# A spiking recommender scan: spikes counted on VectorE instead of TensorE, the comparison fed by ScalarE, item 0's rows made five steps at a time

## The chip, the core and the metric

The kernel runs on one core of one Trainium2 chip. The metric is the device time of one execution in microseconds, the median over several runs. It was 1573.67 us before the change (5 runs, 1573.37 to 1573.87).

## What is computed

There are 1024 sequences (B) of 50 item numbers (T). Each item has a row of D = 128 numbers in a table of 100001 rows. Row 0 counts as zeros.

```python
emb = emb_table.at[0].set(0.0)
prefix = jnp.cumsum(emb[seq], axis=1)
denom = jnp.minimum(arange(1, T + 1)[None, :], lengths[:, None])
uF = prefix / denom[:, :, None]
mean = uF.mean(axis=0)
var = uF.var(axis=0)
y = (uF - mean) * lax.rsqrt(var + 1e-5) * gamma + beta
def step(v, x):                       # over the 50 steps, v starts at 0
    v = v + (x - v) / 2.0
    spike = (v - 1.0 >= 0)
    return v - spike * 1.0, spike
scores = spikes.mean(axis=0) @ emb.T  # 1024 x 100001, float32
```

The output alone is 409.6 MB.

## The kernel before

The kernel has two parts. The first, lines 164 to 406, is the scan over 50 steps. The second, from line 411, multiplies the counts of spikes by the whole table and stores the scores. `tc.manual_schedule()` is in force, so each engine executes its instructions in the order in which the program writes them.

**The scan.** Features lie on the 128 partitions and the 1024 sequences along the free axis. For each step t, `gather` (L191) issues eight indirect DMAs on GpSimd's queue (POOL), 128 rows each, into one of three buffers `e`. It is called two steps ahead: the loop calls `gather(t + 2)`. Eight transposes on TensorE (L301) add the gathered rows to `pre`, two PSUM banks that hold the running sum. Each half (512 sequences) is scaled by VectorE into `uF` (L310), and `bn_stats` (L311) takes its statistics; `bn_aggr` (L321) joins the two halves in `mv`.

Then comes the normalization. ScalarE takes the square root (L325) and subtracts the mean from `uF` in place (L326). VectorE takes the reciprocal `r` (L334), refines it by a Newton step (L336 to L338) and forms the factor `a` (L340). `x` (L344) is a ScalarE operation that writes the scaled input into a new PSUM tile `v`, and `step` (L347) on VectorE subtracts half of the negated old potential `negv`.

The spike of step t - 1 is computed in step t: `s` (L331) is v >= 1 in bfloat16, `negv` (L353) is s - v, and `counted` (L268) adds `s` to two PSUM banks `sums` by two matmuls with an identity. In the last step these are written ahead of everything else (L295, L296), then counted, and `sums` is copied to an SBUF tile `count` (L319).

**Item 0.** Rows of item 0 were gathered and must be taken out of the sum again. `only(t)` (L252, ScalarE) makes a stationary operand `l` that keeps only row t, and `correct(t, l)` (L257) multiplies it by a mask `zT` into `pre`. Step t calls `correct(t + 1, l)` and later `only(t + 2)`.

**The end of the scan.** After the last step sixteen transposes of the identity (`warm`, L378) are put on TensorE's queue ahead of the products. The last membrane step is done in three column groups (L385 to L393), and `spiked` (L279) adds the last spikes to `count` as it writes `countA`, `countB` and `countC`, the stationary operands of the second part. Two first blocks of scores (L397 to L406) are multiplied into `sums` and `po1`, then scaled and stored.

**The second part.** Blocks of the table (1024 rows each) are transposed and split into a high and a low float32r part (`prepare`). Each product needs two matmuls per 512 columns (L152), one eviction by VectorE (L469) or ScalarE (L471), and stores on SyncE's queue. In steps 42 and 44 of the scan the first two blocks are already prepared.

Of the kernel before, what the change touches and what calls it, by code (L numbers as in the profile page):

```python
# [12 lines left out]
F32 = mybir.dt.float32  # L13
BF16 = mybir.dt.bfloat16
F32R = mybir.dt.float32r
I32 = mybir.dt.int32
U32 = mybir.dt.uint32
AF = mybir.ActivationFunctionType
ALU = mybir.AluOpType

P = 128
BN_EPS = 1e-5
V_TH = 1.0
HALF = 1024
KQ = HALF // P
BANK = 512
GROUP = 6
AHEAD = 6
TWICE = 2

WIDTHS = 4 * [2] + 4 * [3] + 13 * [6]
# [4 lines left out]
def rec_kernel(  # L36
# [9 lines left out]
    nc = tc.nc  # L46
    B, T = seq.shape
    N, D = table.shape
# [19 lines left out]
    ident = const.tile([P, P], F32, tag="ident", name="ident")  # L68
# [80 lines left out]
    def product(po, q, n, k0, kw):  # L149
        kw += kw % 2  # L150
        for j, part in enumerate(split[q]):
            nc.tensor.matmul(  # L152
                po[:, :kw],
                lhsT=counts[n],
                rhs=part[:, k0 : k0 + kw],
                start=j == 0,
                stop=j == 1,
            )
# [4 lines left out]

    with ExitStack() as ph:
        once = ph.enter_context(tc.tile_pool(name="once", bufs=1))
        lp = ph.enter_context(tc.tile_pool(name="lif", bufs=2))
        sp = ph.enter_context(tc.tile_pool(name="stats", bufs=3))
        up = ph.enter_context(tc.tile_pool(name="uF", bufs=2))
        gp = ph.enter_context(tc.tile_pool(name="gather", bufs=3))
        accp = ph.enter_context(tc.tile_pool(name="acc", bufs=1, space=bass.MemoryType.PSUM))  # L170
# [8 lines left out]
        gb = once.tile([P, 2], F32, tag="gb", name="gb")  # L179
# [32 lines left out]
        zT = once.tile([P, B], F32R, tag="zT", name="zT")  # L212
# [3 lines left out]
        r0n = once.tile([P, D], F32, tag="r0n", name="r0n")  # L216
# [3 lines left out]
        sel = once.tile([P, P // 2], F32, tag="sel", name="sel")  # L220
# [11 lines left out]
        nc.vector.tensor_copy(rlen, rps)  # L232

        hgb = once.tile([P, 2], F32, tag="hgb", name="hgb")
        nc.vector.tensor_scalar_mul(hgb[:, 0:1], gb[:, 0:1], -0.5)
        nc.vector.tensor_scalar_mul(hgb[:, 1:2], gb[:, 1:2], 0.5)
        eps = once.tile([P, 1], F32, tag="eps", name="eps")
        nc.vector.memset(eps, BN_EPS)
        ident_h = once.tile([P, P], BF16, tag="ident_h", name="ident_h")
        nc.vector.tensor_copy(ident_h, ident)  # L240

        negv = once.tile([P, B], F32, tag="negv", name="negv")
        nc.vector.memset(negv, 0.0)


        pre = [accp.tile([P, BANK], F32, tag=f"pre{h}", name=f"pre{h}") for h in range(B // BANK)]
        sums = [accp.tile([P, BANK], F32, tag=f"sums{h}", name=f"sums{h}") for h in range(B // BANK)]

        def only(t):

            l = sp.tile([P, D], F32R, tag="l", name=f"l_{t}")
            nc.scalar.activation(l, r0n, AF.Copy, scale=sel[:, t : t + 1])  # L252
            return l

        def correct(t, l):
            for h in range(B // BANK):
# [6 lines left out]
                    skip_group_check=True,  # L263
                )

        def counted(t, s):
            for h in range(B // BANK):
                nc.tensor.matmul(  # L268
                    sums[h],
                    lhsT=ident_h,  # L270
                    rhs=s[:, h * BANK : (h + 1) * BANK],
                    start=t == 0,
                    stop=t == T - 2,
                    skip_group_check=True,
                )


        def spiked(out, cs, v):
            nc.vector.scalar_tensor_tensor(out, v, V_TH, count[:, cs], ALU.is_ge, ALU.add)  # L279

        whole = slice(0, B)
        halves = [slice(h * BANK, (h + 1) * BANK) for h in range(B // BANK)]
        v = None

        correct(0, only(0))
        l = only(1)
        gather(1)
        for t in range(T):
            last = t == T - 1
            if t + 2 < T:  # L290
                gather(t + 2)
            e = es.pop(t)
            if last:
                s = lp.tile([P, B], BF16, tag="s", name=f"s_{t - 1}")
                nc.vector.tensor_single_scalar(s, v, V_TH, ALU.is_ge)  # L295
                nc.vector.tensor_tensor(negv, s, v, ALU.subtract)  # L296
            uF = up.tile([P, B], F32, tag="uF", name=f"uF_{t}")
            bs = sp.tile([P, B // BANK, 6], F32, tag="bs", name=f"bs_{t}")
            for h, cs in enumerate(halves):
                for k in range(0, BANK, P):  # L300
                    nc.tensor.matmul(  # L301
                        pre[h][:, k : k + P],
                        lhsT=e[:, h * BANK + k : h * BANK + k + P],
                        rhs=ident,
                        start=False,
                        stop=last,
                        is_transpose=True,
                        skip_group_check=True,
                    )
                nc.vector.scalar_tensor_tensor(uF[:, cs], rlen[:, cs], 1.0 / (t + 1), pre[h], ALU.max, ALU.mult)  # L310
                nc.vector.bn_stats(bs[:, h, :], uF[:, cs])  # L311
            if not last:
                correct(t + 1, l)
            else:

                counted(t - 1, s)
                count = once.tile([P, B], F32, tag="zT", name="count")
                for h, cs in enumerate(halves):
                    nc.scalar.copy(count[:, cs], sums[h])  # L319
            mv = sp.tile([P, 2], F32, tag="mv", name=f"mv_{t}")  # L320
            nc.vector.bn_aggr(mv, bs.rearrange("p h s -> p (h s)"))  # L321


            r = sp.tile([P, 1], F32, tag="r", name=f"r_{t}")
            nc.scalar.activation(r, mv[:, 1:2], AF.Sqrt, bias=eps)  # L325
            nc.scalar.activation(uF, uF, AF.Identity, bias=mv[:, 0:1], scale=-1.0)  # L326


            if t and not last:
                s = lp.tile([P, B], BF16, tag="s", name=f"s_{t - 1}")  # L330
                nc.vector.tensor_single_scalar(s, v, V_TH, ALU.is_ge)  # L331
                counted(t - 1, s)

            nc.vector.reciprocal(r, r)  # L334
            q = sp.tile([P, 1], F32, tag="q", name=f"q_{t}")
            nc.vector.tensor_mul(q, r, r)  # L336
            nc.vector.scalar_tensor_tensor(q, mv[:, 1:2], BN_EPS, q, ALU.add, ALU.mult)
            nc.vector.tensor_scalar(q, q, -0.5, 1.5, ALU.mult, ALU.add)  # L338
            a = sp.tile([P, 1], F32, tag="a", name=f"a_{t}")
            nc.vector.tensor_scalar(a, q, r, hgb[:, 0:1], ALU.mult, ALU.mult)  # L340


            def x(vt, cs):
                nc.scalar.activation(vt, uF[:, cs], AF.Identity, bias=hgb[:, 1:2], scale=a)  # L344

            def step(vt, cs):
                nc.vector.scalar_tensor_tensor(vt, negv[:, cs], -0.5, vt, ALU.mult, ALU.add)  # L347

            if not last:
                vt = vp.tile([P, B], F32, tag=f"v{t % 2}", name=f"v_{t}")  # L350
                x(vt, whole)
                if t:
                    nc.vector.tensor_tensor(negv, s, v, ALU.subtract)  # L353
                step(vt, whole)
                v = vt
                if t + 2 < T:
                    l = only(t + 2)

                if t in (T - 8, T - 6):
                    q = (t - T + 8) // 2  # L360
                    pair(q)
                    prepare(q, vp.tile([P, HALF], F32, tag="v1", name=f"pt_{q}"))
                    if q == TWICE - 1:
                        for k in range(TWICE):
                            rows[GROUP + k] = first[:, k, :]
                        nc.sync.dma_start(
                            out=first[:, :TWICE, :],
                            in_=table[GROUP * HALF : (GROUP + TWICE) * HALF, :].rearrange(
                                "(q p k) d -> p q (k d)", p=P, k=KQ
                            ),  # L370
                        )
# [21 lines left out]
            spiked(c, cs, vt)  # L393


        po1 = vp.tile([P, HALF], F32, tag="v0", name="po_0_1")
        for q, (pool, tag, po) in enumerate(((gp, "e", sums), (up, "uF", [po1[:, cs] for cs in halves]))):  # L397
            o = pool.tile([P, HALF], F32, tag=tag, name=f"o_0_{q}")
            for h, cs in enumerate(halves):
                product(po[h], q, 0, h * BANK, BANK)  # L400
            for h, cs in enumerate(halves):
                if q and h:
                    nc.vector.tensor_scalar_mul(o[:, cs], po[h], 1.0 / T)
                else:
                    nc.scalar.mul(o[:, cs], po[h], 1.0 / T)
                store(0, q * HALF + h * BANK, o[:, cs])  # L406


# [102 lines left out]
```

## Time and profile before

| What | Value |
|---|---|
| median of 5 runs | 1573.67 us (1573.37 to 1573.87) |
| the profiled execution | 1574.11 us |
| its span, first to last instruction | 1572.3 us |
| outside the span | 1.81 us |
| TensorE busy in the span | 1148.2 us (73%) |
| VectorE busy | 941.7 us (60%) |
| ScalarE busy | 631.3 us (40%) |
| GpSimd busy | 378.3 us (24%) |
| mean granted TensorE clock | 0.945 |
| DMA, mean over the span | 310 GB/s |

In the profile's lines PE is TensorE, DVE is VectorE, ACT is ScalarE, POOL is GpSimd and PEld is TensorE's loading of weights. A timeline row gives the start, the duration (both in us), the engine, the line, the operation, output<-input, and in brackets the idle time of that engine just before, with what ended it. A row of a group of instructions gives the total busy time in us and the mean of one in ns, and then the idle time before them. PEclk is the clock granted to TensorE as a share of full speed.

### The profile page before, as it was taken

Reading aid. Unit: us, or ns where it says so; the run is one execution under the profiler, and the core shown is the slowest. Engines: PE = TensorE matmul, PEld = TensorE weight load, DVE = VectorE, ACT = ScalarE, POOL = GpSimd, SP = SyncE. Lnnn points to the kernel's source line nnn. Section 1 sums busy time; section 2 is a strip of 40 time slices with the busy share of each in tenths; the row PEclk is TensorE's granted clock in tenths of the full one; section 3 lists DMA queues with packets and bytes.
Section 4 is the critical chain, followed back from the end, with each engine's and each line's share of the span. In section 5 each row is a group of like instructions: output and inputs, shape, how many; then the busy total and the mean of one; then the engine's idle time right before and its main releaser. Section 6 shows DMA issues by size and latency. Waiting matters only on the chain.

```text
span 1572.3 us, 12553 instructions
## 1 busy us (share of the span) xinstructions
PE 1148.2 (73%) x4538; PEld 818.2 (52%) x4548; DVE 941.7 (60%) x1161; ACT 631.3 (40%) x700; POOL 378.3 (24%) x406
## 2 busy tenths in 40 slices
PE   4555555555546998889888878888788878888884
PEld 2222222222223776668666666666566667666673
DVE  5777777777778665667555545545555545555552
ACT  2322222222233554555444444444344444444542
POOL 7777777777776000000000000000000000000000
PEclk9999999999975999999999999999999999899998
DMA  9611111111121999999999999999999999999997
GB/s 339 247 52 54 52 54 52 54 52 54 52 80 44 385 416 403 423 416 403 419 432 431 430 424 425 417 416 433 425 426 414 408 429 418 419 415 429 406 432 338
DMA packets 53691, 488.14 MB, mean 310 GB/s; under 512 B 11995, under 2 KB 12796, under 8 KB 32380
## 3 DMA queue, kind: packets, MB, share of 16 engines
q1 hardware_dynamic: 32256, 429.81, 65.1%
q0 software_dynamic: 12800, 26.24, 5.7%
q10 hardware_dynamic: 8572, 31.28, 5.0%
q8 instruction: 36, 0.59, 0.1%
q14 instruction: 27, 0.22, 0.0%
HBM read 77.69 MB, written 409.60 MB: 310 GB/s over the span
## 4 chain that ended last, share of the span: by engine, by line
DMA 56%; POOL 17%; PE 9%; issue 8%; ACT 5%; DVE 3%; another core or an unknown queue 0%; ACTq 0%; SPq 0%; DVEq 0%; POOLq 0%
DMA scores<-o 50%; POOL e L194 17%; PE po L152 8%; DMA e<-in_L_rec_emb_table,idx 6%; ACT o L471 5%; DVE o L469 2%; PE pre L301 0%; DVE s L331 0%; DVE bs L311 0%; DVE uF L310 0%; ACT pairs L144 0%; DMA idx<-in_r_seq 0%; PE pt L122 0%; PE sums L268 0%
## 5 line engine op out<-in xcount | busy, mean ns | idle before, releaser
L469 DVE TENSOR_SCALAR o<-po 128x1024 f32<-128x1024 f32 x391 | 464.4, 1221 | 349.6 <-DMA scores<-o 313.5
L471 ACT ACTIVATE o<-po 128x1024 f32<-128x1024 f32 (+1 forms) x391 | 389.2, 1018 | 542.4 <-DMA scores<-o 324.2
L194 POOL DMA_INDIRECT e<-in_L_rec_emb_table,idx x400 | 377.7, 944 | 124.0 <-issue 110.6
L152 PE MATMUL po<-pairs,countB 128*128 128x512 f32 x1136 | 304.3, 414 | 61.4 <-ACT o L471 46.1
L152 PEld LDWEIGHTS po<-pairs,countB 128*128 128x128 f32 x1136 | 217.4, 196 | 124.3 <-ACT o L471 61.2
L152 PE MATMUL po<-pairs,countC 128*128 128x512 f32 x852 | 233.5, 420 | 51.4 <-ACT o L471 51.3
L301 PE MATMUL pre<-ident,e 128*128 128x128 f32 x400 | 156.1, 452 | 151.7 <-DMA e<-in_L_rec_emb_table,idx 148.0
L152 PEld LDWEIGHTS po<-pairs,countC 128*128 128x128 f32 x852 | 164.6, 200 | 96.8 <-ACT o L471 63.4
L301 PEld LDWEIGHTS pre<-ident,e 128*128 128x128 f32 x400 | 79.2, 200 | 245.2 <-DMA e<-in_L_rec_emb_table,idx 222.9
L145 DVE TENSOR_TENSOR pairs<-pt,pairs 128x1024 fp32r<-128x1024 f32 x71 | 86.2, 1222 | 91.7 <-ACT pairs L144 91.6
L325 ACT ACTIVATE r<-mv,eps 128x1 f32<-128x1 f32 x50 | 14.8, 295 | 305.5 <-DVE mv L321 305.5
L310 DVE SCALAR_TENSOR_TENSOR uF<-rlen,pre 128x512 f32<-128x512 f32 x100 | 68.4, 684 | 108.3 <-PE pre L301 108.2
L122 PE MATMUL pt<-ident,rows 128*128 128x128 f32 x782 | 111.4, 289 | 5.3 <-issue 3.2
L122 PEld LDWEIGHTS pt<-ident,rows 128*128 128x128 f32 x782 | 100.8, 152 | 24.1 <-issue 9.4
L152 PE MATMUL po<-hi,countB 128*128 128x512 f32 x216 | 88.8, 411 | 19.9 <-ACT o L471 14.9
L257 PE MATMUL pre<-zT,l 128*128 128x512 f32 x100 | 77.4, 776 | 19.5 <-DVE uF L310 19.3
L268 PE MATMUL sums<-s,ident_h 128*128 128x512 bf16 x88 | 45.3, 606 | 61.0 <-DVE s L331 61.0
L152 PE MATMUL po<-lo,countB 128*128 128x512 f32 x216 | 85.9, 399 | 0.0
L152 PE MATMUL po<-hi,countC 128*128 128x512 f32 (+1 forms) x162 | 68.6, 423 | 15.0 <-ACT o L471 15.0
L144 ACT CAST pairs<-pt 128x1024 fp32r<-128x1024 f32 x71 | 71.8, 1012 | 14.1 <-PE pt L122 13.9
L152 PE MATMUL po<-pairs,countA 128*128 128x512 f32 x284 | 71.0, 393 | 6.2 <-ACT o L471 6.2
L344 ACT ACTIVATE v<-uF,hgb,a 128x1024 f32<-128x1024 f32 x49 | 59.2, 1208 | 37.4 <-DVE a L340 37.4
(76 smaller groups left out, 844.3 us busy)
## 6 DMA issues: line engine op xcount, KB each, us to landing
scores<-o SPq DMA_DIRECT2D x96, 3072.0 KB, 20.3
scores<-o SPq DMA_DIRECT2D x32, 1536.0 KB, 8.9
scores<-o SPq DMA_DIRECT2D x30, 1024.0 KB, 8.6
rows<-in_L_rec_emb_table ACTq DMA_DIRECT2D x19, 1536.0 KB, 29.1
scores<-o SPq DMA_DIRECT2D x8, 2896.5 KB, 17.2
rows<-in_L_rec_emb_table SPq DMA_DIRECT2D x6, 3072.0 KB, 30.2
e<-in_L_rec_emb_table,idx POOLq DMA_INDIRECT x400, 2.5
rows<-in_L_rec_emb_table SPq DMA_DIRECT2D x1, 1024.0 KB, 5.3
```

The costliest lines, as they stand in the source:

```text
L122: nc.tensor.transpose(pt[:, k0 : k0 + kw], r[:kw, k0 : k0 + D], ident[:kw, :kw])
L144: nc.scalar.copy(vh, vp)
L145: nc.vector.tensor_tensor(vl, vp, vh.bitcast(F32), ALU.subtract)
L152: nc.tensor.matmul(po[:, :kw], lhsT=counts[n], rhs=part[:, k0 : k0 + kw], start=j == 0, stop=j == 1,)
L194: nc.gpsimd.indirect_dma_start(out=es[t][:, n * P : (n + 1) * P], out_offset=None, in_=table, in_offset=bass.IndirectOffsetOnAxis(ap=idx[: ...
L257: nc.tensor.matmul(pre[h], lhsT=l, rhs=zT[:, h * BANK : (h + 1) * BANK], start=t == 0, stop=False, skip_group_check=True,)
L268: nc.tensor.matmul(sums[h], lhsT=ident_h, rhs=s[:, h * BANK : (h + 1) * BANK], start=t == 0, stop=t == T - 2, skip_group_check=True,)
L301: nc.tensor.matmul(pre[h][:, k : k + P], lhsT=e[:, h * BANK + k : h * BANK + k + P], rhs=ident, start=False, stop=last, is_transpose=True, ...
L310: nc.vector.scalar_tensor_tensor(uF[:, cs], rlen[:, cs], 1.0 / (t + 1), pre[h], ALU.max, ALU.mult)
L344: nc.scalar.activation(vt, uF[:, cs], AF.Identity, bias=hgb[:, 1:2], scale=a)
L469: nc.vector.tensor_scalar_mul(o[:, h0 : h0 + hw], po[:, :hw], 1.0 / T)
L471: nc.scalar.mul(o[:, h0 : h0 + hw], po[:, :hw], 1.0 / T)
```

## The change

VectorE counts the spikes with a running sum in bfloat16 (`count`), by an operation in every step, where two matmuls added them to PSUM. ScalarE writes d = v - 1 in bfloat16 after each membrane step (`over`), and VectorE forms `negv` from d and v in one operation (`rest`); the tile `s` is gone. `only` makes the operands of five steps in one VectorE operation. The Newton step has one operation less. The first block of scores goes into a new two-bank PSUM tile `po0` in place of `sums`.

```diff
+ONLY = 5
-        lp = ph.enter_context(tc.tile_pool(name="lif", bufs=2))
+        lp = ph.enter_context(tc.tile_pool(name="lif", bufs=1))
-        nc.vector.tensor_scalar_mul(hgb[:, 0:1], gb[:, 0:1], -0.5)
+        nc.vector.tensor_scalar_mul(hgb[:, 0:1], gb[:, 0:1], 0.25)
-        ident_h = once.tile([P, P], BF16, tag="ident_h", name="ident_h")
-        nc.vector.tensor_copy(ident_h, ident)
+        less = once.tile([P, 1], F32, tag="less", name="less")
+        nc.vector.memset(less, -V_TH)
+        count = once.tile([P, B], BF16, tag="count", name="count")
+        nc.vector.memset(count, 0.0)
-        sums = [accp.tile([P, BANK], F32, ...) for h in range(B // BANK)]
+        ls = once.tile([P, ONLY, D], F32R, tag="ls", name="ls")
         def only(t):
-            l = sp.tile([P, D], F32R, tag="l", name=f"l_{t}")
-            nc.scalar.activation(l, r0n, AF.Copy, scale=sel[:, t : t + 1])
-            return l
+            k = t % ONLY
+            if k == 0:
+                n = min(ONLY, T - t)
+                nc.vector.tensor_tensor(
+                    ls[:, :n, :],
+                    r0n.unsqueeze(1).to_broadcast([P, n, D]),
+                    sel[:, t : t + n].unsqueeze(2).to_broadcast([P, n, D]),
+                    ALU.mult,
+                )
+            return ls[:, k, :]
-        def counted(t, s):        # two matmuls with ident_h into sums
+        def over(t, v):
+            d = lp.tile([P, B], BF16, tag="d", name=f"d_{t}")
+            nc.scalar.activation(d, v, AF.Identity, bias=less)
+            return d
+        def rest(d, v):
+            nc.vector.scalar_tensor_tensor(negv, d, 0.0, v, ALU.is_ge, ALU.subtract)
             if last:
-                s = lp.tile([P, B], BF16, tag="s", name=f"s_{t - 1}")
-                nc.vector.tensor_single_scalar(s, v, V_TH, ALU.is_ge)
-                nc.vector.tensor_tensor(negv, s, v, ALU.subtract)
+                rest(d, v)
+                spiked(count, whole, v)
...
-            else:
-                counted(t - 1, s)
-                count = once.tile([P, B], F32, tag="zT", name="count")
-                for h, cs in enumerate(halves):
-                    nc.scalar.copy(count[:, cs], sums[h])
...
             if t and not last:
-                s = lp.tile([P, B], BF16, tag="s", name=f"s_{t - 1}")
-                nc.vector.tensor_single_scalar(s, v, V_TH, ALU.is_ge)
-                counted(t - 1, s)
+                rest(d, v)
             nc.vector.reciprocal(r, r)
             q = sp.tile([P, 1], F32, tag="q", name=f"q_{t}")
-            nc.vector.tensor_mul(q, r, r)
-            nc.vector.scalar_tensor_tensor(q, mv[:, 1:2], BN_EPS, q, ALU.add, ALU.mult)
-            nc.vector.tensor_scalar(q, q, -0.5, 1.5, ALU.mult, ALU.add)
+            nc.vector.scalar_tensor_tensor(q, mv[:, 1:2], BN_EPS, r, ALU.add, ALU.mult)
+            nc.vector.tensor_scalar(q, q, r, 3.0, ALU.mult, ALU.subtract)
...
                 x(vt, whole)
                 if t:
-                    nc.vector.tensor_tensor(negv, s, v, ALU.subtract)
+                    spiked(count, whole, v)
                 step(vt, whole)
                 v = vt
+                d = over(t, v)
                 if t + 2 < T:
                     l = only(t + 2)
...
+        po0 = accp.tile([P, HALF], F32, tag="po0", name="po_0_0")
         po1 = vp.tile([P, HALF], F32, tag="v0", name="po_0_1")
-        for q, (pool, tag, po) in enumerate(((gp, "e", sums), (up, "uF", [po1[:, cs] for cs in halves]))):
+        for q, (pool, tag, po) in enumerate(((gp, "e", po0), (up, "uF", po1))):
```

## The prediction

> **What bounds the kernel now.** I read the slices of the span first, to part the stages.
>
> ```profile
> POOL 7777777777776000000000000000000000000000
> PEclk9999999999975999999999999999999999899998
> DMA  9611111111121999999999999999999999999997
> ```
>
> A slice is 39.3 us. GpSimd works for the first 12.8 slices, the scan, and never again; from then on the DMA engines are full to the end. The second part starts when the scan's counts are ready and nothing in it is changed, so the time moves by what the scan's end moves, and by what the first products lose or gain.
>
> Then I read, within the scan, the groups of instructions and the waits from 100 to 400 us, which are 30 steps.
>
> ```profile
> L194 POOL DMA_INDIRECT e<-in_L_rec_emb_table,idx x241 | 227.4, 944 | 73.4 <-issue 68.3 <-DMA e<-in_L_rec_emb_table,idx 5.2
> DVE uF L310 <- PE pre L301: 71.8, 30, 2.5
> ACT r L325 <- DVE mv L321: 190.3, 30, 6.4
> ```
>
> One gather takes 0.944 us and 0.30 us of gap (73.4 / 241), never more than 0.31: GpSimd waits for nobody. Eight make 9.99 us, and 300 / 30 is 10.0 us per step. VectorE instead stands still once per step, for 71.8 / 30 = 2.4 us, until the second half's gathers have landed and been transposed. So the scan runs at the gathers' pace, and the others have 2.4 us to spare per step. The gathers end at 502.06 + 0.95 = 503.0 us. Only what follows is bound by the other engines; that is VectorE's timeline over the end of the scan.
>
> ```profile
> 498.68 1.21 DVE L353 TENSOR_TENSOR negv<-s,v 128x1024 f32<-128x1024 bf16 x1
> 500.10 1.23 DVE L347 SCALAR_TENSOR_TENSOR v<-negv,v 128x1024 f32<-128x1024 f32 x1 [0.21 <-ACT v L344]
> 501.36 1.23 DVE L295 TENSOR_SCALAR s<-v 128x1024 bf16<-128x1024 f32 x1
> 502.62 1.22 DVE L296 TENSOR_TENSOR negv<-s,v 128x1024 f32<-128x1024 bf16 x1
> 503.76 0.68 DVE L310 SCALAR_TENSOR_TENSOR uF<-rlen,pre 128x512 f32<-128x512 f32 x1
> 504.47 0.69 DVE L311 BATCH_NORM_STATS2 bs<-uF 128x6 f32<-128x512 f32 x1
> 505.10 0.69 DVE L310 SCALAR_TENSOR_TENSOR uF<-rlen,pre 128x512 f32<-128x512 f32 x1
> ```
>
> From 500.10 VectorE has no pause. The last gather's transpose runs at 504.58 for 0.47 us, and the second uF starts at 505.10: here gathers and VectorE tie, with nothing to spare.
>
> **The change part by part.**
>
> *Steady steps.* VectorE loses s (1.17 us) and negv (1.21) and gains `rest` and `spiked`, each like L347 (1.23); one Newton operation goes (0.16, 0.19 with its gap); `only` adds one operation on 640 elements per five steps. The nearest rows, both with two SBUF inputs, took 0.225 us for 64 elements and 0.289 for 128, 1 ns per element, so 0.225 + 576 x 0.001 = 0.80 us, or 0.16 per step. The sum per step is 1.23 + 1.23 + 0.16 - 1.17 - 1.21 - 0.19 = +0.05 us against 2.4 spare. ScalarE loses `only` (0.39) and gains `over`, from PSUM to SBUF like L471 (1.02; at most 1.21 as L344): +0.6 us, and it idles 6.3 us per step; d is there about 4 us before `rest` needs it. TensorE loses two 0.61 us matmuls that nobody waited for. With `only`'s 0.80 us between step and uF, VectorE still reaches the second half 1.5 us early. The gathers' buffers are three, so GpSimd has a step in hand. All of this costs nothing as long as the gathers set the pace; without that cover it would be the 0.05 us x 49 = 2.5 us on VectorE.
>
> *Setup.* `only(0)` moves behind VectorE's setup: that ends at 14.33 us, a memset (at most 0.91) and 0.80 us later is 16.1, and TensorE's first transposes queue behind `correct(0)`, from 11.96 to about 17.3. The first step gets some 0.8 us late; it takes that from the 3.08 us that VectorE waits in the next. No gather waits for it: the first that needs buffer e_0 free is issued at 33.95.
>
> *The last step.* `rest` waits for d, and d for `over` of the membrane step just made. Behind `rest` on VectorE's queue stand `spiked`, both uF and both statistics. Before, s could follow step at once (501.36). Now ScalarE starts at 501.33 + 0.05, d is ready at 502.40 by L471's 1.02 (502.6 by L344's 1.21), and `rest` starts at 502.45: +1.09. `rest` and `spiked` take what s and negv took. Newton's shortening gives back about 0.05 in step 48 (against a `rest` 0.06 longer than s) and at most 0.14 in step 49, where x then waits for ScalarE's own L326 (to 508.12, x at 508.26); I take 0.1. The copies of `sums` (505.52 to 506.59) were over before the square root's input came (506.76): nothing from them. The counts come 1.09 - 0.15 = **+0.95 us** later (0.9 to 1.2).
>
> *The first products and the clock.* This is the uncertain term. The view is TensorE's busy time and clock by stretches.
>
> ```profile
> 441.00:445.00 4.00, 3.32 (x16) 1.00 0.16 49
> 445.00:449.00 4.00, 1.29 (x4) 1.00 0.24 65
> 449.00:500.00 51.00, 28.03 (x73) 0.50 0.24 73
> 505.20:508.90 3.70, 3.70 (x17) 0.50 0.00 0
> 508.90:510.40 1.50, 1.30 (x4) 0.50 0.00 0
> 510.40:515.00 4.60, 4.09 (x18) 1.00 0.61 228
> ```
>
> The third figure from the right is the clock. It fell after a thin stretch (1.29 busy of 4 us, around the first prepared block, whose wait on TensorE's queue stays). In 51 us at 28.03 / 51 = 55% busy it did not come back. It came back at 510.4, after 5.15 us of warm-up and products with hardly a gap, from 505.28. In the new kernel warm starts at about 505.1 (the matmuls in front of it are gone) and ends at 508.7, but the products start at 510.47: a pause of 1.75 us that was 0.2. By the nearest row (5.15 us of continuous work) counted from 510.47, the clock is back at 515.6. At half clock the first matmuls followed each other by 0.56 and 0.40 us, at full by 0.23. Eight matmuls of the first two blocks at 0.40 to 0.48 end at 513.8 to 514.6; then one ScalarE eviction (0.60) and one VectorE eviction (0.69), for which TensorE waited also before (until 513.42): it goes on at 515.2 to 516.0, that is +1.8 to +2.6, the 0.95 included. From there to 525.8, where the stores take over, TensorE is busy all the time, so this passes on whole. I take **+2.2**. The other end, a clock that is up when the products start: 0.95 less the 0.5 that three slow matmuls lost before, +0.45.
>
> [...]
>
> `po0` as one tile may make its first eviction wait for both banks: 0 to 0.47 us, but the eviction of `po1` comes after it anyway and sets the pace. I take 0.
>
> Sum: 0 in the steps, 0.95 + 1.25 = +2.2 us. The profiled execution would go from 1574.11 to 1576.3. It lay 0.44 over the median, so the median goes from 1573.67 to 1575.9.
>
> **The rivals.** About 0.2% (3.15 us) is what a measurement of this kernel can tell from no change.
>
> *1, slower: the five-step operation holds up the gathers.* It reads two SBUF operands while GpSimd works, which no VectorE operation of a steady step does. In the setup some do.
>
> ```profile
> 7.87 0.29 DVE L219 TENSOR_TENSOR r0n<-r0hi,r 64x128 f32<-64x128 f32 x1
> 8.94 0.76 DVE L227 COPY rb<-rl 128x1024 f32<-128x1024 f32 x1
> ...
> 7.73 0.94 POOL L194 DMA_INDIRECT e<-in_L_rec_emb_table,idx  x1 [0.30 <-issue]
> 8.98 0.94 POOL L194 DMA_INDIRECT e<-in_L_rec_emb_table,idx  x1 [0.30 <-issue]
> 10.23 0.94 POOL L194 DMA_INDIRECT e<-in_L_rec_emb_table,idx  x1 [0.30 <-issue]
> ```
>
> Both ran inside a gather, and the gathers kept 0.94 us and their 1.25 us pitch. Only the very first gather (1.16 us, beside L208) is 0.22 longer. So I take 0. If each of the ten operations stalls GpSimd by 0.22 to 0.80 us, the scan ends 2.2 to 8.0 later: +4.4 to +10.2. It decides from 0.1 us per operation.
>
> [...]
>
> *2, slower: the clock stays low longer.* If it needs as much again after 515.6 (5.15 us at half), TensorE loses some 2.5 more: +4.7. For it: 55% busy did not bring it back. Against it: the products leave few gaps.
>
> *3, within 0.2%: the clock never falls,* because the transposes no longer queue behind counting matmuls and spread evenly: +0.45, or 1574.1. Against it stands the thin stretch before 449.
>
> **How the numbers follow.** Forecast 0.60, rival 1 0.14, rival 2 0.10, rival 3 0.13, and 0.03 for a gain of more than 3.15 us, for which I see no row. Same is 0.60 + 0.13 = 0.73, slower 0.14 + 0.10 = 0.24, faster 0.03. The range runs from rival 3 less the runs' spread (0.2), 1573.9, to rival 2, 1578.4; outside lie the 0.03 and most of rival 1.
>
> **What would show it.** Right: the gathers' pitch of 1.25 us unchanged to 503 us; L310's wait still about 2 us per step; an idle time of about 1.1 us on VectorE before the last `rest`, ended by ScalarE; countA 0.95 us later; a clock of 0.5 at the first products and a step back between 513 and 517. Wrong: gathers longer or farther apart beside the five-step operation; the clock at 1.0 at 510; a scan that ends before 508.

## The result, and the profile after

The changed kernel takes 1577.43 us (median of 22 runs, 1576.68 to 1578.56), the kernel before in the same study 1573.83 (42 runs, 1573.26 to 1575.12): a ratio of 1.0023, 95% interval 1.0017 to 1.0029. It is slower, by 3.6 us, and the interval reaches to both sides of the 0.2% (3.15 us) that the prediction named as the least that can be told. The profiled execution of the changed kernel ("after" from here on) took 1577.62 us with a span of 1575.8, 3.5 more than before's 1572.3.

The slices first, as in the prediction.

```profile
POOL 7777777777776000000000000000000000000000
PEclk9999999999995999999999999999999999999998
```

The picture is the same: the scan in 12.8 slices, then stores to the end. So the 3.5 us must come from the scan and the first products. The steady steps, from 100 to 400 us, by groups and by waits:

```profile
L195 POOL DMA_INDIRECT e<-in_L_rec_emb_table,idx x241 | 227.5, 944 | 73.4 <-issue 68.0 <-DMA e<-in_L_rec_emb_table,idx 5.5
...
L284 DVE SCALAR_TENSOR_TENSOR negv<-d,v 128x1024 f32<-128x1024 bf16 x31 | 36.2, 1167 | 0.0
```

```profile
DVE uF L317 <- PE pre L308: 71.6, 30, 2.6
```

A gather still takes 944 ns and its gap 73.4 / 241 = 0.30 us, VectorE still waits 71.6 / 30 = 2.4 us per step for the transposes, and `negv` has no idle time ahead of it (0.0): `d` is always there. The mean of 100 to 400 us says that nothing happened. The row of all 400 gathers says otherwise in one figure, the longest (after "ns": least, median, longest):

```profile
L195 POOL DMA_INDIRECT e<-in_L_rec_emb_table,idx x400: 940/944/2252, 4.0 to 504.4; - x134
```

Before, the longest was 1163 ns and the last started at 502.06. So I put the two profiled executions side by side by four moments:

| us | before | after | difference |
|---|---|---|---|
| first gather starts | 3.77 | 3.98 | +0.21 |
| from first to last gather's start | 498.29 | 500.46 | **+2.17** |
| from last gather's start to first product | 7.46 | 8.28 | **+0.82** |
| from first product to the end of the span | 1062.8 | 1063.1 | +0.3 |
| span | 1572.3 | 1575.8 | +3.5 |

The first row is GpSimd's wait for the item numbers (2.46 us before, 2.67 after); in the other traces here the first gather starts anywhere between 3.91 and 4.25 us, and nothing of the change stands ahead of it on its queue, so I count it as spread.

Three gathers make the second row. They are found in the timeline of GpSimd and VectorE where the five-step operation (`ls`, L258) runs (start, duration, engine, line; the bracket is idle time just before).

```profile
14.20 2.25 POOL L195 DMA_INDIRECT e<-in_L_rec_emb_table,idx  x1 [0.30 <-issue]
14.88 0.76 DVE L258 TENSOR_TENSOR ls<-r0n,sel 128x640 fp32r<-128x640 f32 x1
...
56.35 0.82 DVE L258 TENSOR_TENSOR ls<-r0n,sel 128x640 fp32r<-128x640 f32 x1
56.69 1.30 POOL L195 DMA_INDIRECT e<-in_L_rec_emb_table,idx  x1 [0.30 <-issue]
...
103.23 0.94 POOL L195 DMA_INDIRECT e<-in_L_rec_emb_table,idx  x1 [0.30 <-issue]
103.57 0.82 DVE L258 TENSOR_TENSOR ls<-r0n,sel 128x640 fp32r<-128x640 f32 x1
104.48 0.94 POOL L195 DMA_INDIRECT e<-in_L_rec_emb_table,idx  x1 [0.30 <-issue]
...
455.06 0.82 DVE L258 TENSOR_TENSOR ls<-r0n,sel 128x640 fp32r<-128x640 f32 x1
455.31 1.39 POOL L195 DMA_INDIRECT e<-in_L_rec_emb_table,idx  x1 [0.30 <-issue]
```

At 56.69 and 455.31 a gather started while the operation was running. It then lasted to that operation's end plus 0.82 us: 57.17 - 56.69 + 0.82 = 1.30, and 455.88 - 455.31 + 0.82 = 1.39. At 103.57 the operation started 0.34 into a gather: that gather kept 0.94, the operation kept 0.82, and the next gather, which began 0.09 after the operation's end, kept 0.94 too. The six other operations lie like this one, 0.30 to 0.40 us into a gather. The extra is (2.25 + 1.30 + 1.39) - 3 x 0.94 = 2.12 of the 2.17 us.

The last step, on VectorE's timeline:

```profile
502.41 1.23 DVE L345 SCALAR_TENSOR_TENSOR v<-negv,v 128x1024 f32<-128x1024 f32 x1 [0.20 <-ACT v L342]
504.82 1.22 DVE L284 SCALAR_TENSOR_TENSOR negv<-d,v 128x1024 f32<-128x1024 bf16 x1 [1.18 <-ACT d L280]
505.95 1.22 DVE L287 SCALAR_TENSOR_TENSOR count<-v,count 128x1024 bf16<-128x1024 f32 x1
```

VectorE stands for 1.18 us after the membrane step, released by ScalarE's `d`, where before it went on at once. And TensorE around the first products, by stretches (busy time and number of matmuls, granted clock, DMA share, GB/s):

```profile
507.20:510.50 3.30, 3.30 (x17) 0.58 0.00 0
510.50:512.70 2.20, 0.01 (x1) 1.00 0.00 0
...
513.40:516.60 3.20, 3.20 (x10) 0.50 0.28 106
516.60:520.00 3.40, 3.39 (x15) 0.97 0.74 283
```

The warm-up ends at 510.52 and the products start at 512.72: the pause is 2.20 us (1.75 forecast, 0.20 before). But the clock rose already within the warm-up (0.58 on average there) and was full when the products started; it fell at 513.4, behind three of them, and came back at 516.8 (the 0.97 of the last row is 0.2 us at half).

### The profile page after: what moved, and what is told of

Its sections match the earlier page's. It is cut to its first block, busy times and chain, and to the rows that moved or that the text cites. A ratio compares the mean times of both kernels' runs of the same rounds, so it can differ in the third digit from the quotient of the medians.

```text
span 1575.8 us, 12231 instructions
## 1 busy us (share of the span) xinstructions
PE 1126.2 (71%) x4450; PEld 797.2 (51%) x4450; DVE 944.5 (60%) x1122; ACT 668.1 (42%) x697; POOL 380.5 (24%) x406
## 4 chain that ended last, share of the span: by engine, by line
DMA 52%; POOL 18%; PE 12%; issue 8%; ACT 6%; DVE 2%; another core or an unknown queue 0%; ACTq 0%; POOLq 0%; DVEq 0%; SPq 0%
DMA scores<-o 47%; POOL e L195 18%; PE po L153 11%; DMA e<-in_L_rec_emb_table,idx 6%; ACT o L471 5%; DVE o L469 1%; ACT pairs L145 0%; PE pt L123 0%; DVE pairs L146 0%; DMA idx<-in_r_seq 0%; PE pre L308 0%; DVE negv L284 0%; DVE bs L318 0%; DVE uF L317 0%
## 5 line engine op out<-in xcount | busy, mean ns | idle before, releaser
L308 PE MATMUL pre<-ident,e 128*128 128x128 f32 x400 | 181.0, 464 | 228.4 <-DMA e<-in_L_rec_emb_table,idx 228.0
L308 PEld LDWEIGHTS pre<-ident,e 128*128 128x128 f32 x400 | 73.5, 185 | 339.0 <-DMA e<-in_L_rec_emb_table,idx 338.3
L268 PE MATMUL pre<-zT,ls 128*128 128x512 f32 x100 | 78.1, 783 | 22.5 <-DVE uF L317 18.7
L280 ACT ACTIVATE d<-v,less 128x1024 bf16<-128x1024 f32 x49 | 54.5, 1113 | 63.6 <-DVE v L345 63.6
```

The source lines that it names most:

```text
L268: nc.tensor.matmul(pre[h], lhsT=l, rhs=zT[:, h * BANK : (h + 1) * BANK], start=t == 0, stop=False, skip_group_check=True,)
L280: nc.scalar.activation(d, v, AF.Identity, bias=less)
L308: nc.tensor.matmul(pre[h][:, k : k + P], lhsT=e[:, h * BANK + k : h * BANK + k + P], rhs=ident, start=False, stop=last, is_transpose=True, ...
```

## The experiments

**What had to be told apart.** My theory after the result: the five-step operation, because it reads two operands from SBUF, holds any gather that starts while it runs, and this is the 2.17 us; the last step's wait for `d` is the 0.82; the clock at the first products adds some 0 to 2 us that differ from run to run. The rivals: the long gathers come from something else in the change (the setup's extra memsets, `over`, the counting), or any operation of that length holds a gather; and the last step's 0.82 is the order of the two VectorE operations, not the wait.

All runs of one group share runs of the kernel before, and the groups fell on three chips. e1 to e4 ran on one where the kernel before takes 1573.91 us, e11 and e12 on another where it takes 1573.73. e5 to e10 ran on a third, where it takes 1651.56 and 1652.34 (two groups); this one is called the 1652 us chip below. Most of the difference stands in GpSimd's timeline there, in each of the six traces from it, here of e6_twice_psum:

```profile
60.44 0.94 POOL L195 DMA_INDIRECT e<-in_L_rec_emb_table,idx  x1 [6.68 <-remote]
```

About every 45 us GpSimd stops, mostly for some 5.5 us (6.68 the first time), twelve to fourteen times in the scan, and the last gather starts near 566 us. That is 19 us or more ahead of the first product (in e5 565.37 and 586.33), where in after it is 8.28: on that chip the scan's end does not wait for the gathers, and long gathers can go unpaid. Runs of one kernel spread there by up to 10 us. From that chip I read traces only; the times are given, and nothing is concluded from them.

**e1_only_act.** After, with before's `only`: one ScalarE operation per step, and no long VectorE operation with two SBUF inputs in the scan.

```diff
-        ls = once.tile([P, ONLY, D], F32R, tag="ls", name="ls")
...
-                nc.vector.tensor_tensor(ls[:, :n, :], r0n..., sel..., ALU.mult)
-            return ls[:, k, :]
+            l = sp.tile([P, D], F32R, tag="l", name=f"l_{t}")
+            nc.scalar.activation(l, r0n, AF.Copy, scale=sel[:, t : t + 1])
+            return l
```

> The changed kernel with item 0's rows made one step at a time by ScalarE again, as before; all else as changed. Theory (the five-step operation on VectorE, with two SBUF inputs, holds gathers back): the three long gathers (2.25, 1.30, 1.39 us) are gone, all 400 last 0.94 us except the first, the last starts at about 502.1 to 502.3 instead of 504.44, and the time falls by about 2.1 us against the changed kernel, to some 1.4 us above the kernel before. Rival (something else in the new steps holds the gathers: the running count, or ScalarE's bfloat16 write): long gathers stay and the time stays at that of the changed kernel.

1575.70 us (ratio 1.0010, 1.0001 to 1.0019). The longest gather has 1164 ns (1163 before), and the gathers take 498.31 us from first to last start, as before's 498.29. Everything else of the change is in this kernel, the memset of the setup too. So neither that nor `over` nor the counting makes gathers long. The first product starts 8.24 us behind the last gather's start, as in after.

**e2_only_alone.** Before, with after's five-step operation alone.

```diff
+ONLY = 5
...
-            nc.scalar.activation(l, r0n, AF.Copy, scale=sel[:, t : t + 1])
...
+                nc.vector.tensor_tensor(ls[:, :n, :], r0n..., sel..., ALU.mult)
```

> The kernel before with the five-step operation of item 0's rows alone. Theory: some gathers get longer, those of which the start falls inside the operation, each by (end of the operation minus start of the gather plus 0.82) minus 0.94 us; 0.4 to 4 us in all, and the time rises by as much. Rival (the rest of the change holds the gathers): all gathers at 0.94 us and the time of the kernel before.

1575.44 us (1.0009, 1.0000 to 1.0018). Two gathers are long, 1.85 us at 14.40 and 1.41 at 56.53, and the gathers take 499.74, that is 1.45 more than before. From the last gather to the first product it is 7.57 (before 7.46), and the clock is full there. The operation alone costs time by holding gathers; two of ten places were hit here, three in after. In seven of the others it started about 0.5 us into a gather. There its end reached 0.06 to 0.11 us into the next gather, which shows no hold: 0.11 + 0.82 is 0.93, less than the 0.94 of a free one. In the tenth it started 0.02 us into a gather and did nothing to it:

```profile
455.27 0.94 POOL L195 DMA_INDIRECT e<-in_L_rec_emb_table,idx  x1 [0.30 <-issue]
455.29 0.83 DVE L257 TENSOR_TENSOR ls<-r0n,sel 128x640 fp32r<-128x640 f32 x1
```

**e3_swap_last** and **e4_both.** After (e3) and e1 (e4), with the count ahead of `negv` in the last step. If only `negv` waits for `d`, the count fills the wait.

```diff
             if last:
-                rest(d, v)
-                spiked(count, whole, v)
+                spiked(count, whole, v)
+                rest(d, v)
```

> The changed kernel with the two first VectorE operations of the last step in the other order: the count, which needs only v, ahead of negv, which needs d. Theory (the last step waits for ScalarE's d): the 1.18 us wait of VectorE before the last negv falls to about 0, countA comes 1.1 us earlier against the last gather, and the time falls by 0.7 to 1.5 us, as the clock of the first products falls. Rival (the wait is covered by the gathers, which end 2.4 us later here): the count ends no earlier, because the last transposes at 506.9 set the second uF; time unchanged.

> The changed kernel with both: item 0's rows on ScalarE, and the count ahead of negv in the last step. Theory: 2.1 + 1.1 us less than the changed kernel, so within 0.6 us of the kernel before on either side; countA within 0.2 us of the 509.09 of the kernel before. Rival (the clock of the first products, at half for 3.4 us there, is the larger part): still over 1 us slower than before.

e3 took 1578.40 us (1.0028, 1.0016 to 1.0039), e4 1575.28 (1.0009, 1.0000 to 1.0018): the swap brought nothing against after and e1. That is a miss, and VectorE's timeline of e4 has the reason.

```profile
500.18 1.23 DVE L336 SCALAR_TENSOR_TENSOR v<-negv,v 128x1024 f32<-128x1024 f32 x1 [0.20 <-ACT v L333]
502.59 1.23 DVE L278 SCALAR_TENSOR_TENSOR count<-v,count 128x1024 bf16<-128x1024 f32 x1 [1.18 <-ACT d L271]
```

The same 1.18 us now stand ahead of the count, which does not use `d`. It reads the PSUM tile `v` that ScalarE is reading for `d`, and starts when ScalarE has done. So the order of the two is not what costs. That ScalarE reads `v` first is the explanation left, and the next run tries it.

**e7_last_own.** e4, with the last step's spike taken by VectorE from `v`, as in before; `d` isn't made in step 48, and the spikes are added to the count behind `bn_aggr`.

```diff
             if last:
-                spiked(count, whole, v)
-                rest(d, v)
+                s = lp.tile([P, B], BF16, tag="d", name="s")
+                nc.vector.tensor_single_scalar(s, v, V_TH, ALU.is_ge)
+                nc.vector.tensor_tensor(negv, s, v, ALU.subtract)
...
+            if last:
+                nc.vector.tensor_tensor(count, count, s, ALU.add)
...
-                d = over(t, v)
+                if t + 2 < T:
+                    d = over(t, v)
```

> As the run with both (rows of item 0 on ScalarE), but VectorE makes its own comparison in the last step, as before the change: s and negv from v, and the count takes s (bfloat16, both operands in SBUF) after the statistics. ScalarE writes no d for step 48. Theory (the last step waits 1.18 us for ScalarE to read v): the wait is gone, countA comes 7.0 to 7.4 us after the last gather's start instead of 7.84, and the time falls by 0.4 to 0.8 us against the run with both. Rival (the gathers' landing sets the second uF anyway): countA stays at 7.84.

1650.61 us beside before's 1652.34 on that chip (0.9986, 0.9971 to 1.0000). In its trace the wait is gone:

```profile
577.46 1.23 DVE L339 SCALAR_TENSOR_TENSOR v<-negv,v 128x1024 f32<-128x1024 f32 x1 [0.20 <-ACT v L336]
578.73 1.22 DVE L294 TENSOR_SCALAR s<-v 128x1024 bf16<-128x1024 f32 x1
...
586.41 0.29 DVE L278 SCALAR_TENSOR_TENSOR countA<-pre,count 128x128 fp32r<-128x128 f32 x1
```

From the step's end (578.69) to countA it is 7.72 us; in e8, on the same chip and with `d`, 8.64, as in after (503.64 to 512.28); in before 7.76. So the wait for `d` costs 0.92, and taking ScalarE off `v` gives all of it back. Whether it would show in the time of a chip on which before takes 1574 us wasn't run.

**e5_twice and e12_twice** are one kernel, run on the 1652 us chip (e5) and on one where before takes 1573.73 us (e12): after, with the five-step operation made twice in a row wherever it stands in the scan.

```diff
-                nc.vector.tensor_tensor(ls[:, :n, :], r0n..., sel..., ALU.mult)
+                for _ in range(2 if t else 1):
+                    nc.vector.tensor_tensor(ls[:, :n, :], r0n..., sel..., ALU.mult)
```

**e6_twice_psum and e11_once_psum** put the first operand into PSUM, so that the same operation reads one operand from SBUF; e6 on top of e5, e11 on top of after.

```diff
+        r0p = accp.tile([P, D], F32, tag="po0", name="r0p")
+        nc.vector.tensor_copy(r0p, r0n)
-                    r0n.unsqueeze(1).to_broadcast([P, n, D]),
+                    r0p.unsqueeze(1).to_broadcast([P, n, D]),
```

> The changed kernel with the five-step operation issued twice, one behind the other, in each of its nine places in the scan (once in the setup). Theory (an operation with two SBUF inputs blocks a gather that starts inside it, until it ends; then the gather needs 0.82 us more): in most places the operation ended 1.14 us after a gather's start and missed the next one's, at 1.25; the second copy ends at about 1.93 and now holds the next gather for about 0.56 us. Nine places make some 4 to 6 us more of gather time than in the changed kernel, and the time rises by as much. Rival (VectorE's queue is only busier; the three long gathers have another cause): 0.8 us more VectorE work per five steps, covered by the 2.5 us wait per step; the time of the changed kernel.

> As the run with the operation issued twice, but its first input is a copy of the rows in PSUM, in the two banks that the first block of scores takes at the end, so that only one of the inputs lies in SBUF. Theory (two SBUF inputs are what blocks): all gathers at 0.94 us but the first, the last starts at about 502.2, and the time is 2 us below the changed kernel in spite of the doubled work. Rival (any VectorE operation at that place does it): as slow as the run with two SBUF inputs.

> The changed kernel with the first input of the five-step operation in PSUM: the same operation at the same places on VectorE, with one SBUF input. Theory (two SBUF inputs hold gathers that start inside the operation): no long gather but the first, the last one starts at about 502.2 instead of 504.4, and the time falls by about 2 us against the changed kernel. Rival (where the operation stands on VectorE is what counts, not where its inputs lie): as the changed kernel.

> The changed kernel with the five-step operation issued twice in a row, once more, since on the chip of the first run GpSimd also waited some 60 us for other reasons, which covers small delays. Theory, as read there (a gather that starts inside a copy lasts until that copy's end and 0.82 us more; it gets in between the two copies): each of the nine places that ended at 1.14 us after a gather's start now has its second copy over the next gather's start (1.25), and holds it by up to 0.6 us: 3 to 5 us more gather time than the changed kernel, and the time rises by as much. Rival: the time of the changed kernel.

e12 took 1580.28 us (5 runs; 1.0035, 1.0022 to 1.0049) and e11 1575.78 (1.0014, 1.0005 to 1.0023), with before at 1573.73. In e11 the operation is as long as in after. Gathers start inside it, 0.39 us behind its start here and 0.18 at 453.89, and they aren't held; e11's gathers take 498.34 us:

```profile
55.25 0.82 DVE L260 TENSOR_TENSOR ls<-r0p,sel 128x640 fp32r<-128x640 f32 x1
55.64 0.94 POOL L195 DMA_INDIRECT e<-in_L_rec_emb_table,idx  x1 [0.30 <-issue]
```

That is the experiment that decides: the same engine, the same length, the same place in the order (but for the copy into PSUM in the setup), one operand moved, and 2.1 of the 2.17 us are back. In e12 six gathers are long (the very first of all, 1.16 us in every trace, is left out here and below), and the gathers take 502.27, 1.81 more than after; 3 to 5 were expected. Five of the nine pairs in the scan held a gather, where two single operations did in after. One of them, with the two copies as one row:

```profile
153.69 1.68 DVE L259 TENSOR_TENSOR ls<-r0n,sel 128x640 fp32r<-128x640 f32 x2
154.60 1.59 POOL L195 DMA_INDIRECT e<-in_L_rec_emb_table,idx  x1 [0.30 <-issue]
```

The gather starts 0.91 into the pair, that is within the second copy, and its 1.59 us reach to the pair's end plus 0.82 (155.37 - 154.60 + 0.82), as with the single operation. In e5 (1649.52 beside 1651.56; 0.9988, 0.9978 to 0.9998) ten gathers are long, and the nine in the scan last 0.97 to 1.50; each reaches to the end of the copy that was running when it started, plus 0.82. A gather held by the first copy doesn't wait for the second as well; it gets in between them (e12: 1.24 us at 56.93 and 1.41 at 457.35, where the pair's end plus 0.82 would have made 2.11 and 2.27). So doubling the operation gave it more places to hit, not a higher price for a hit. The time did not rise by the 4 to 6 us that were expected of e5, and on that chip it says nothing for or against. In e6 (1651.15; 1.0000, 0.9990 to 1.0009) no gather of the scan is long, though in all eight pairs between 73 and 475 us one starts inside.

**e10_setup_early.** After, with the operation for the first five steps put right behind the setup of `sel`, ahead of the memsets.

```diff
+        l0 = only(0)
...
-        correct(0, only(0))
+        correct(0, l0)
```

> The changed kernel with the five-step operation of the setup moved ahead, behind the making of sel, so that it doesn't follow the two memsets. Theory (the gather of 2.25 us was held by that operation, from before its own recorded start, while the memset in front of it still ran): that gather lasts 0.94 us, another one in the setup gets at most 0.3 us longer, the scan ends 1.0 to 1.3 us earlier, and so does the kernel. Rival (the memsets hold it): it stays at 2.25.

1651.50 us (before 1652.34; 0.9991, 0.9981 to 1.0001).

```profile
8.92 0.82 DVE L232 TENSOR_TENSOR ls<-r0n,sel 128x640 fp32r<-128x640 f32 x1
9.46 1.45 POOL L195 DMA_INDIRECT e<-in_L_rec_emb_table,idx  x1 [0.30 <-issue]
```

The hold moved with the operation. The gather beside the memset of `negv` (14.97) is free again, with 0.94, so the memset alone holds nothing. The setup's loss went from 1.31 to 0.51 us. In the scan of this trace seven gathers are long (0.97 to 1.58 us), each to the operation's end plus 0.82, and two rows show how near the edge lies: an operation that started 0.05 us ahead of a gather (414.21 and 414.26) held it for 1.58 us, one that started 0.02 ahead (240.48 and 240.50) left it at 0.94 and itself took 0.87.

Two things stay open, both in the setup. By the rule of the scan the gather at 9.46 should last 1.10, not 1.45. And in after the gather at 14.20 started 0.68 ahead of the operation's record, with the memset of `negv` (14.05 to 14.96) in front of it; by that rule it should not have been held at all, yet its 2.25 are again the operation's end plus 0.81. In e2 it is the same with 0.29 (gather 14.40, operation 14.69).

**e8_warm22 and e9_own_warm20.** e4 with 22 warm-up transposes, e7 with 20 (both had 16), to shorten the pause ahead of the products.

```diff
-        for k in range(2 * KQ):
+        for k in range(22):
```

> As the run with both, with 22 warm-up transposes instead of 16, so that TensorE is busy from 505.1 to about 510.1 and the products start without a pause. Theory (the pause of 1.7 us keeps the clock at half for the first 3.5 us of products): the clock is up at or before the first products, which then follow each other by 0.23 us instead of 0.43, the third block starts at about 514 instead of 515.5, and the median falls by 1 to 1.6 us. Rival (the clock's step falls at chance, or the evictions set the pace): less than 0.4 us.

> As the run with its own comparison in the last step, with 20 warm-up transposes. Theory: both gains together, 0.5 to 1.0 us below the kernel before, since its first three products also ran at half clock (0.5 us) and the Newton step is shorter. Rival: the gains overlap, and the time is that of the kernel before or above.

1654.85 us for e8 (1.0008, 0.9992 to 1.0025) and 1651.56 for e9 (0.9995, 0.9981 to 1.0008), before 1652.34. The warm-up lasted 4.2 us in e8 and 4.5 in e9, the pause 1.17 and 0.96. The first products then, as stretches of TensorE, of e8 and of e9:

```profile
586.00:588.00 2.00, 1.97 (x9) 1.00 0.00 0
```

```profile
592.10:595.60 3.50, 3.49 (x8) 0.50 0.00 0
```

With the shorter pause and the longer stretch of work the clock of e9 stayed at half; e8's was full. One trace of each cannot say what more warm-up is worth, and the times of that chip can't either. What it says is that neither the pause nor the length of the warm-up decides alone. In the traces from the chips on which before takes 1574 us, with 16 warm-ups, it goes the same way:

| profiled execution | pause, us | clock at the first products | first product to end of span, us |
|---|---|---|---|
| before | 0.20 | half for three products | 1062.8 |
| e2_only_alone | 0.69 | full | 1062.3 |
| e11_once_psum | 1.82 | full | 1062.35 |
| e3_swap_last | 2.12 | full, then half from 513.7 to 517.1 | 1062.9 |
| after | 2.20 | full, then half from 513.4 to 516.8 | 1063.1 |
| e4_both | 1.68 | half for some 3.5 us | 1063.8 |
| e12_twice | 1.82 | half for some 3 us | 1063.9 |
| e1_only_act | 1.73 | half for some 3.4 us | 1064.2 |

A clock that stays at half for the first 3 to 3.5 us of products costs 1.5 to 1.9 us against a full one (1063.8 to 1064.2 in the last column, against 1062.3). The runs fit with such a draw, though they don't prove it: kernels with the long pause lie within 1.9 us (after), 2.2 (e1, e11) and 2.1 (e4) of each other, before and e2, with the short one, within 1.0 and 0.7 us in the same group as e1 and e4, but before's 42 runs of the first study within 1.9 us too.

What is drawn can be read from the traces. In before and in after all 59 steps of the clock lie whole multiples of 3.41 us apart, and two steps are never closer than one such length: in before 448.99 and 510.43 (18 of them), in after 509.98, 513.39 and 516.81 (one each). In e3 the three steps at the first products, 510.26, 513.66 and 517.08 by the mean clocks of its stretches of 1 us, lie 3.40 and 3.42 apart. So I took the work of TensorE in the 3.41 us before each rise at the end of the scan, and before the moments that lie whole multiples of 3.41 us from it. e11 and e12 have the same warm-up (3.67 us) and the same pause (1.82). In e11 the clock rose at 509.79, and the 3.41 us before held 2.75 us of TensorE work. In e12 it rose only at 517.85, with 2.98 us of work before it; at 511.03 and 514.44, with 2.48 and 2.02 before them, it stayed at half. Over the eight traces, from 500 to 518 us, all ten rises had 2.75 us or more before them, and the moments that passed at half clock had 2.70 at most (e1, 507.54). That is no sharp limit: in after, 2.73 us of work (469.02 to 472.43) and 2.82 (1435.00 to 1438.41) at half clock weren't followed by a rise. What makes a full clock fall is not settled by these rows, and no run shifted these moments on purpose.

## Why the prediction was right, and where a step of it failed

The time lies in the range and the sign of the sum is right, but it forecast +2.2 us, 0.14%, and got +3.6. The likeliest case held for the part it described; a share of rival 1 came on top. That the time still lies in the range is in part luck: its upper end was there for rival 2, a clock that stays at half for longer, and that did not come; it was rival 1, which the range mostly left out, that filled the place. And two of the signs that were named for being wrong appeared: longer gathers beside the five-step operation, and a clock of 1.0 at 510 (after's rose at 509.98).

- *Steady steps: 0.* Right. The cover held: between the long gathers their pitch and VectorE's wait are unchanged. The sizes were 1.17 for `rest`, 1.21 for the count, 0.82 for the five-step operation (0.80 forecast), 1.11 for `over` (1.02 taken, 1.21 as the upper end).
- *The five-step operation holds no gather: 0.* Wrong; this is the step that failed, by +2.17. The rows that I used could not show it. The two-input operations of the setup (L219, L221) began 0.14 and 0.46 us after a gather's start, and runs here show that in the scan a start inside a gather harms neither (0.02 us into it in e2, 0.30 to 0.40 in after). L227 did not run inside a gather, as I wrote; it began 0.04 us ahead of one, and it reads one SBUF operand. Nor is it so that no VectorE operation of a steady step reads two SBUF operands: L336 and L337 do, on one element per partition. L337 at 488.21 to 488.37 even lies over the start of a gather, at 488.34, but its end plus 0.82 is 0.85 us behind that start, less than the 0.95 that the gather took. The row that was needed, two SBUF inputs for longer over the start of a gather, isn't in before's trace, so the bound from that side was 0.22 to 0.80 per operation, and I gave it too little weight. Rival 1 had the mechanism but a wrong count: it let all ten operations cost. Where one starts is tied to the gathers by the transposes, for which VectorE waits in every step (71.6 us in 30 steps), and seven of the ten fell 0.30 to 0.40 us into a gather, out of harm's way; two fell over a gather's start, and the one in the setup held a gather too. The lower end of rival 1, +4.4, was above the result.
- *What a hit cost.* The rows at 56.69 and 455.31 and e11 speak against what I took. An operation that starts 0.34 into a gather (103.57) wasn't blocked by it (0.82 us, as ever) and didn't block it (0.94). By the rows of the scan the hold is decided when the gather starts, and a hit in the scan cost 0.36 and 0.45 us in after and 0.66 at most (e12), not the operation's whole 0.82.
- *Setup: 0.* Wrong for the same reason: whatever the first step's lateness cost was covered, but the operation held a gather there for 1.31 us, the largest of the three.
- *The last step: +0.95.* Right: +0.82 in after, +0.72 to +0.93 in the others with `d` where before takes 1574 us, 0.92 in e7 against e8. The wait is 1.18 (1.09 forecast; `d` took 1.11, not 1.02).
- *The first products: +1.25, or -0.5 with the clock up.* Both ends right in size: +1.0 (e4) and +1.4 (e1) with the clock at half, -0.45 (e11) with it full. Which of them came, the prediction could not know: in these traces the clock rose with 2.75 us of TensorE work in the 3.41 us before 509.79 (e11), and not with 2.48 before 511.03 (e12); I took one end for the likeliest. The 5.15 us of work without a gap that I took for the price of the full clock were too much: after's clock rose with 3.07 us of work in the 3.41 before, e11's with 2.75, and with the clock at half it was back at 513.96 (e4) and 514.36 (e1), not at 515.6. After's own profiled run went a third way, full, then half for 3.4 us, and lost 0.3.
- *`po0` and Newton: 0 and -0.1.* Nothing in the traces speaks against them; they weren't tried alone. In the last step the rows from the reciprocal to `a` start 0.65 us apart in after and 0.77 before, so Newton's shortening is 0.12 there; one of the two operations left got longer (0.21 us, 0.15 before).

Taken together, e11, which is the change without the holds, costs 1575.78 - 1573.73 = 2.05 us: near the 2.2 that the sum had forecast for everything else. No version beat the kernel before on the chips where it takes 1574 us; the nearest was e4 with +1.4 us. e7, which has neither the holds nor the wait for `d`, is the one that would have to be timed there.

## What to carry to other kernels

When an engine's fixed pace is the bound, ask of each operation put beside it not only whether there is time, but whether the paced instruction gets longer where the two overlap (0.94 us became 1.30 and 1.39 here, and stayed 0.94 with one operand in PSUM), and look in the trace for a row with the same operands over the *start* of the paced instruction; a row a tenth of a microsecond to the side proves little (L219, 0.14 us behind a gather's start). The mean of a long stretch hides three long instructions in 400: read the longest of a group, not its mean. And work that is moved off an engine's queue may leave a pause there, and behind the same pause of 1.82 us the clock was full in one execution (e11) and at half in another (e12): price both outcomes.

## What was not expected of the hardware

- A VectorE operation with both operands in SBUF delays, in the scan, an indirect gather that starts inside it to the operation's end plus 0.82 us (a free one takes 0.94; one that started 0.02 us behind the operation's start, in e10, kept that too); an operation that starts inside the gather does nothing to it (0.02 us into it in e2, 0.30 to 0.40 in seven places of after). With one of the operands in PSUM no gather was held (e11, e6). In the setup gathers were held past this rule (after, e2, e10), which is open.
- An operation that only reads a PSUM tile was still held until the other engine's reading of it was over: the count ahead of `negv` in e4, 1.18 us. Whether the chip does this or an order that was put into the program, no run shows.
- Another chip ran the unchanged kernel in 1652 us instead of 1574. The changed kernels' traces from it show pauses of some 5.5 us in GpSimd's gathers about every 45 us; what they are is open. There the changed kernels come out level with the kernel before or slightly ahead, between 0.9986 and 1.0008 in ratio, for which I have no reason, so that the same change can look different by the chip that it lands on.
- TensorE 55% busy at half clock (before, 449 to 500 us) didn't get its clock back, and TensorE 47% busy at full clock (after, 4.20 of 9 us from 440 to 449, clock 1.00) didn't lose it there; it lost it at 469.0. All 59 steps of the clock in before, and all 59 in after, lay whole multiples of 3.41 us apart.
